# Choosing experts' tokens: gate bias and division by the sum moved from passes over 4096 tokens to columns and to the experts' answers

## The chip, the cores and the metric

The kernel runs on one core of one Trainium2 chip. The metric is the device time of one execution in microseconds (us); lower is better. The kernel before took 10838.91 us, the median of three runs (10834.52 to 10853.2). Everything is in float32.

## The reference, cut to what matters

Four images of 128 channels and 64 x 64 pixels pass through a convolution and scan layer, a convolution, an attention layer with an expert layer, and a second attention layer with a second expert layer. The change lies in the expert layers alone (`f2` and `f3` in the kernel). Each has 64 experts; every expert chooses 8 of the 4096 tokens of each image.

```
logits = einsum('bsd,ed->bse', x, gate_w) + gate_b          # x is the layer-normed token
probs  = softmax(logits, axis=1)                            # over the 4096 tokens
vals, idx = top_k(probs.transpose(0, 2, 1), 8)              # per image and expert
pooled = einsum('bked,bke->bed', gathered, topv)            # weighted sum of the 8 tokens
out    = two layers with gelu per expert, on pooled
outputs[token] += out * topv                                # added back to the 8 tokens
```

The softmax runs over tokens, so a gate bias, one number per expert, is the same for all the values that one softmax compares.

## The kernel before, in words

Images are kept as `xs[b]`, 128 channels (partitions) by 4096 tokens. `expert_ffn` works on pairs of images: a tile `picks[pr]` of 128 x 4096 holds, in its lower and upper 64 partitions, the 64 experts' logits for the two images of pair `pr`. For each of the two pairs there are three steps.

- `weigh(pr)` makes the layer norm's column scale `rs` and the logits, 512 tokens at a time, with TensorE (PE), ScalarE (ACT) and VectorE (DVE). Its last operation of each chunk writes `pick` (L1434).
- `choose(pr)` is nine operations of VectorE and one of ScalarE, each over the whole tile or over one column: add the gate bias (L1441), the eight largest (MAX8, L1443), the negated maximum `nmx` (L1445), the exponential with its sum `tot` on ScalarE (L1447), the reciprocal `rt` (L1449), the multiplication by `rt` (L1450), the eight largest again (L1452), a copy with these eight set to zero (L1454), the difference, which leaves the eight chosen weights (L1455), and their product with the token scale `rs` as `pick_rs` (L1456).
- `collect(pr)` turns `pick_rs` and the two images' tokens with TensorE transposes (L1468, tile `tok_t`), copies them out of PSUM (L1471 on VectorE, L1473 on ScalarE) and sums the weighted tokens into `pool`.

The order is `run(weigh(0)); choose(0); run(weigh(1), collect(0)); choose(1); run(collect(1))`; where two steps stand in one `run`, their chunks are interleaved. Then 16 groups of four experts follow (`hidden`, `turn_hidden`, `answer`, `place`), with 2 MB of weights per group, two groups held at a time, loaded by the SP queue (L1364, L1367). The sum of the answers, `out_ps`, is copied to `out_s` (L1555), and TensorE multiplies `out_s` with the chosen weights in `pick` and VectorE adds the result to the image (L1563). [...] Layer 3's attention lies between the two expert layers, and the output transfers follow the second.

## Time and profile before

One profiled execution took 10849.6 us by its own time; its span, from the first to the last instruction, is 10847.5 us. It is 10.7 us above the median of the three runs.

| stretch of the span (us) | work | length (us) | PE busy | DVE busy | TensorE clock |
|---|---|---|---|---|---|
| 0 to 9640 | layers 0 and 1, most of layer 2's attention | 9640 | 8190 | 7033 | 0.83 to 1.00 |
| 9769.0 to 9801.8 | f2, choose(0) | 32.8 | 0.0 | 27.2 | 0.54 |
| 9801.8 to 9868.1 | f2, weigh(1) and collect(0) | 66.3 | 59.5 | 38.0 | 0.97 |
| 9868.1 to 9899.6 | f2, choose(1) | 31.5 | 0.1 | 27.2 | 0.54 |
| 9927.0 to 10042.0 | f2, 16 expert groups | 115.0 | 94.5 | 16.3 | 0.79 |
| 10060.5 to 10482.0 | layer 3's attention | 421.5 | 300.4 | 252.9 | 0.91 |
| 10537.2 to 10570.0 | f3, choose(0) | 32.8 | 0.0 | 27.3 | 0.54 |
| 10570.0 to 10636.0 | f3, weigh(1) and collect(0) | 66.0 | 59.4 | 38.1 | 0.97 |
| 10636.0 to 10667.4 | f3, choose(1) | 31.4 | 0.0 | 27.2 | 0.54 |
| 10695.0 to 10815.0 | f3, 16 expert groups | 120.0 | 96.5 | 16.5 | 0.77 |

Busy times are sums over the instructions of one engine in the stretch. The TensorE clock is the share of full speed that was granted. In a timeline a row is: start, duration, engine, line, operation, output <- inputs, shapes, count, and in brackets how long the engine stood idle before it and what ended that.

### The profile page before, as it was taken

How to read it: one execution, taken by the hardware profiler on the slowest of the kernel's cores; microseconds unless marked ns; L12 is line 12 of the kernel's file. 1: busy time of each engine (PE TensorE's matmuls, PEld its weight loads, DVE VectorE, ACT ScalarE, POOL GpSimd, SP SyncE). 2: the span in 40 equal slices, each digit the busy share in tenths (PEclk: the TensorE clock that was granted, in tenths of full speed). 3: DMA queues.
4: the chain of work that ended last, by engine and by line, in shares of the span. 5: the costliest groups of instructions: out<-in, count | busy, mean ns of one | idle time of the engine just before them, and what ended most of it. 6: DMA issues, size and time to landing. Idle time of an engine off the chain costs nothing. (4 is left out here: it accounts for less than half of the span.)

```text
span 10847.5 us, 184105 instructions
## 1 busy us (share of the span) xinstructions
PE 9021.2 (83%) x71952; PEld 3473.1 (32%) x71952; DVE 7647.7 (71%) x8462; ACT 7513.2 (69%) x10317; POOL 5239.0 (48%) x3143
## 2 busy tenths in 40 slices
PE   5777778777866999978999978999978999976767
PEld 2123323322342333333333333333333333323433
DVE  2787677668856777767777767777767777754563
ACT  2665575565526999967999968999958999942431
POOL 1565555556634655645566635666635665520000
PEclk8788878878878999989999989999989999987888
DMA  3322322321212112222221122222222212223004
GB/s 81 88 70 56 89 73 55 86 75 50 62 60 49 34 33 36 37 68 44 33 38 35 33 71 42 38 35 34 33 75 42 35 34 33 33 89 105 6 17 140
DMA packets 524325, 581.58 MB, mean 54 GB/s; under 512 B 106232, under 2 KB 329536, under 8 KB 520896
## 3 DMA queue, kind: packets, MB, share of 16 engines
q1 hardware_dynamic: 523456, 569.81, 22.9%
q8 instruction: 568, 9.31, 0.4%
q14 instruction: 301, 2.47, 0.1%
HBM read 373.96 MB, written 76.55 MB: 42 GB/s over the span
## 5 line engine op out<-in xcount | busy, mean ns | idle before, releaser
L1208 ACT ACTIVATE ex<-score 128x1024 f32<-128x1024 f32 x5120 | 4934.2, 1033 | 469.8 <-PE score L90 180.1
L90 PE MATMUL ctx_ps<-ex,qt 128*32 128x512 f32 x20480 | 2719.4, 595 | 0.0
L1155 POOL TENSOR_TENSOR folded<-ex 128x1024 f32<-128x1024 f32 x704 | 1679.6, 2386 | 2074.2 <-ACT ex L1208 2054.2
L1214 DVE STREAM_TRANSPOSE turned<-ex 128x1024 f32<-128x1024 f32 x1536 | 1879.5, 1224 | 491.5 <-ACT ex L1208 428.1
L90 PE MATMUL acc_ps<-turned,turned_v 128*32 128x256 f32 x24576 | 1826.2, 388 | 181.4 <-DVE turned L1194 179.6
L1194 DVE STREAM_TRANSPOSE turned<-ex 128x1024 f32<-128x1024 f32 x1536 | 1854.0, 1207 | 0.0
L90 PE MATMUL score<-queries,keys 32*128 32x512 f32 x10240 | 1358.3, 496 | 140.7 <-ACT ex L1208 81.0
L687 DVE TENSOR_TENSOR_SCAN hs<-decay,carry,hs 128x512 f32<-128x512 f32 x1024 | 1252.8, 1266 | 197.3 <-ACT decay L686 183.0
L686 ACT ACTIVATE decay<-dt,a_neg 128x512 f32<-128x512 f32 x1024 | 700.9, 689 | 794.3 <-DVE hs L687 772.6
L90 PEld LDWEIGHTS score<-queries,keys 32*128 32x128 f32 x10240 | 524.3, 182 | 2196.0 <-issue 1666.2
L693 POOL TENSOR_TENSOR hs<-hs,c_sb 128x1024 f32<-128x1024 f32 x512 | 1205.1, 2375 | 43.5 <-DMA c_sb<-c_d 24.0
L1156 POOL TENSOR_TENSOR quarters<-folded 128x512 f32<-128x512 f32 x704 | 905.4, 1286 | 55.2
L90 PEld LDWEIGHTS acc_ps<-turned,turned_v 128*32 128x32 f32 x24576 | 561.6, 108 | 897.8 <-issue 555.8
L90 PEld LDWEIGHTS ctx_ps<-ex,qt 128*32 128x32 f32 x20480 | 684.5, 109 | 461.4 <-DVE ctx L1137 53.1
L90 PE MATMUL y_ps<-hs,pair 128*64 128x512 f32 x2048 | 652.3, 761 | 138.6 <-POOL hs L693 138.5
L683 DVE TENSOR_TENSOR hs<-dtx,b_ps 128x2048 f32<-128x2048 f32 x256 | 582.3, 2275 | 261.8 <-PE b_ps L90 177.1
L1137 DVE COPY ctx<-ctx_ps 128x512 f32<-128x512 f32 x256 | 177.0, 692 | 669.8 <-PE ctx_ps L90 669.8
L690 POOL COPY carry<-hs 128x4 f32<-128x4 f32 x256 | 59.8, 234 | 1028.0 <-DVE hs L687 990.5
L1027 POOL TENSOR_TENSOR turned_v<-v,quarter 128x1024 f32<-128x1024 f32 x192 | 459.5, 2394 | 17.4 <-ACT ex L1208 11.1
L1201 DVE TENSOR_REDUCE dacc<-quarters 128x2 f32<-128x512 f32 x704 | 453.2, 644 | 7.2 <-POOL quarters L1156 7.2
L90 PE MATMUL b_ps<-dbc,spread 32*128 32x512 f32 x512 | 322.3, 712 | 64.5 <-DVE hs L683 64.4
L1208 ACT ACTIVATION_READ_ACCUMULATOR ex<-score 128x1 f32 x1664 | 348.7, 210 | 0.0
(353 smaller groups left out, 9574.1 us busy)
## 6 DMA issues: line engine op xcount, KB each, us to landing
c_sb<-c_d SPq DMA_DIRECT2D x512, 128.0 KB
queries<-head_d SPq DMA_DIRECT2D x1024, 64.0 KB
keys<-head_d SPq DMA_DIRECT2D x1024, 64.0 KB
dt<-dt SPq DMA_DIRECT2D x128, 256.0 KB
dtx<-dtx SPq DMA_DIRECT2D x128, 256.0 KB
w<-in_L_ffn_weight SPq DMA_DIRECT2D x32, 1024.0 KB
w<-in_L_ffn_weight SPq DMA_DIRECT2D x128, 256.0 KB
under<-xp SPq DMA_DIRECT2D x384, 66.0 KB
```

The source lines that it names most:

```text
L90: self.nc.tensor.matmul(out, lhsT, rhs, start=start, stop=stop)
L683: nc.vector.tensor_tensor(hs, dtx2, bb.unsqueeze(1).to_broadcast([P, NQ, CH]), ALU.mult)
L686: nc.scalar.activation(ex, dt2[:, q, :], AF.Exp, scale=a_neg[:, q, g : g + 1])
L687: nc.vector.tensor_tensor_scan(hs[:, q, :], ex, hs[:, q, :], carry[:, g, q : q + 1], ALU.mult, ALU.add)
L693: nc.gpsimd.tensor_tensor(at, at, cs.unsqueeze(1).to_broadcast([P, 2, CH]), ALU.mult)
L1027: nc.gpsimd.tensor_tensor(t, v.unsqueeze(2).to_broadcast([P, 4 * BT, 4, HD]), quarter.unsqueeze(1).to_broadcast([P, 4 * BT, 4, HD]), ALU.mult,
L1155: nc.gpsimd.tensor_tensor(hs, exs[:, :, 0], exs[:, :, 1], ALU.add)
L1156: nc.gpsimd.tensor_tensor(qs, hs[:, :, 0 : CH // 2], hs[:, :, CH // 2 :], ALU.add)
L1194: nc.vector.transpose(*upright)
L1201: nc.vector.tensor_reduce(at, qs, AX.X, ALU.add)
L1208: nc.scalar.activation(ex, sps[p], AF.Exp, scale=scale, accum_out=dacc[:, j, h, t : t + 1] if summed else None)
L1214: nc.vector.transpose(*upright)
```

## The change

Three things are edited, all in `expert_ffn`. The pass that adds the gate bias over 128 x 4096 goes; the bias enters the column `nmx` instead, which becomes -(top + bias) by one operation with two steps and then has the bias added by a new one. The pass that multiplies 128 x 4096 exponentials by `rt` goes; the second MAX8, the replacement and the difference work on undivided exponentials. `rt` is kept per pair (in the pool `tok`, under a name per pair) and is multiplied in at two places: in `pick_rs`, whose product of two tensors becomes a product with a column and a tensor, and at the copy of the answers' sum into `out_s`.

```diff
         def choose(pr):
 
             pb, rs = picks[pr], parts[pr]
-            nc.vector.tensor_scalar(pb, pb, gate_b, None, ALU.add)
             top = work.tile([P, 8], F32, name="top")
             nc.vector.max(top, pb)
             nmx = work.tile([P, 1], F32, name="nmx")
-            nc.vector.tensor_scalar(nmx, top[:, 0:1], -1.0, None, ALU.mult)
+            nc.vector.tensor_scalar(nmx, top[:, 0:1], gate_b, -1.0, ALU.add, ALU.mult)
+            nc.vector.tensor_tensor(nmx, nmx, gate_b, ALU.add)
             tot = work.tile([P, 1], F32, name="tot")
             nc.scalar.activation(pb, pb, AF.Exp, bias=nmx, accum_out=tot)
-            rt = work.tile([P, 1], F32, name="rt")
+            rt = tok.tile([P, 1], F32, name=f"rt{pr}")
             nc.vector.reciprocal(rt, tot)
-            nc.vector.tensor_scalar(pb, pb, rt, None, ALU.mult)
+            scales.append(rt)
             top = work.tile([P, 8], F32, name="top")
             nc.vector.max(top, pb)
             ws = parts[pr] = tok.tile([P, L], F32, name="pick_rs")
             nc.vector.match_replace(ws, top, pb, 0.0)
             nc.vector.tensor_tensor(pb, pb, ws, ALU.subtract)
-            nc.vector.tensor_tensor(ws, pb, rs, ALU.mult)
+            nc.vector.scalar_tensor_tensor(ws, pb, rt, rs, ALU.mult, ALU.mult)
...
             os_ = work.tile([P, P], F32, name="out_s")
-            nc.vector.tensor_copy(os_, ops[pr])
+            nc.vector.tensor_scalar(os_, ops[pr], scales[pr], None, ALU.mult)
```

On every other engine and queue the instructions and their order are those of before; on VectorE only the rows shown differ. The tiles of the pool `work` in the two expert layers lie 64 bytes further on.

## The prediction

> **What bounds the kernel here.** I read the waits of TensorE (PE) after layer 2 first, then the stretches of the four choices, then the first of them instruction by instruction, then the chain of work that ended last, and last the rows that price the new operations. The waits, as engine, line and awaited engine, then total us, times, longest:

> ```profile
> PE tok_t L1468 <- DVE pick_rs L1456: 134.1, 4, 33.7
> PE hid_ps L90 <- DMA w<-in_L_ffn_weight: 39.3, 13, 5.1
> ```

> PE stands 33 us at each of four places until `pick_rs` is written. By stretch (busy PE, PEld, DVE, ACT, POOL, granted clock, DMA share, GB/s), nothing runs beside VectorE (DVE) there but ScalarE's exponential:

> ```profile
> 9769.00:9801.80 32.80, 0.00 (x0) 0.03 (x1) 27.21 (x10) 5.08 (x3) 0.00 (x0) 0.54 0.00 0
> 9868.10:9899.60 31.50, 0.08 (x1) 0.08 (x2) 27.23 (x11) 3.80 (x2) 0.00 (x0) 0.54 0.00 0
> ```

> The first choice in order of time; the reader is to see that each row starts when the one before ends, that the only gap is ScalarE's, and that PE starts 0.14 us after the last row ends:

> ```profile
> 9769.00 2.35 DVE L1441 TENSOR_SCALAR pick<-pick,gate_b 128x4096 f32<-128x4096 f32 x1
> 9771.39 4.43 DVE L1443 MAX8 top<-pick 128x8 f32<-128x4096 f32 x1
> 9775.85 0.15 DVE L1445 TENSOR_SCALAR nmx<-top 128x1 f32<-128x1 f32 x1
> 9781.20 0.16 DVE L1449 RECIPROCAL rt<-tot 128x1 f32<-128x1 f32 x1 [5.20 <-ACT pick L1447]
> 9781.40 2.35 DVE L1450 TENSOR_SCALAR pick<-pick,rt 128x4096 f32<-128x4096 f32 x1
> 9783.79 4.43 DVE L1452 MAX8 top<-pick 128x8 f32<-128x4096 f32 x1
> ...
> 9797.23 4.42 DVE L1456 TENSOR_TENSOR pick_rs<-pick,rs 128x4096 f32<-128x4096 f32 x1
> 9801.80 1.08 PE L1468 MATMUL tok_t<-ident,pick_rs 128*128 128x128 f32 x4 [33.70 <-DVE pick_rs L1456]
> ```

> The chain that ended last passes through the two later choices in the same rows; of the last one:

> ```profile
> 10636.03 2.36 DVE pick L1441
> 10638.42 4.44 DVE top L1443
> 10643.07 3.81 ACT pick L1447 x2
> 10647.10 2.37 DVE pick L1450
> 10649.49 4.44 DVE top L1452
> ```

> The chain that is shown begins at 10062.7, so for the two choices of f2 the place on the path is inferred from PE's wait, not read. So the choices' DVE work is serial, and what it loses should move all that follows.

> **Removed.** Two passes per choice. From start to start, L1441 takes 9771.39 - 9769.00 = 2.39 us and L1450 9783.79 - 9781.40 = 2.39; the last choice gives 2.39 for both too. Per choice 4.78, four choices 19.12 us. L1450 gone starts MAX8 straight after the reciprocal, which already waits for ScalarE, so no new wait appears. L1441 gone makes the first MAX8 wait for L1434, on the same engine, just before it. The wait for `gate_b`'s transfers moves to `nmx`; they landed before PE's first matmul of the stage, over 50 us earlier.

> **Added, per choice.**

> - `nmx` gets a column as its scalar instead of a number. The 128x1 rows with a column (layer norm's `gn_v`, median 219 ns) and without (`gn_off`, 158 ns) differ by 0.06 us; I take that. Ends 0 and 0.06.
> - A new 128x1 sum of two columns. `gn_d`, a TENSOR_TENSOR of this size, has median 144 ns; the reciprocal's row shows 0.04 between its end and the next start (9781.20 + 0.16 to 9781.40). So 0.18; ends 0.14 and 0.22. ScalarE's exponential, and in the first choice of each layer its 1.28 us table load, wait for `nmx` and start 0.24 later.
> - L1456 becomes a pass with a column and two tensors. No row has it at 4096. At 128x512 from PSUM, `nrm` (two tensors) is 691 ns and `ln_rs` (column and two tensors) 751 at the median: +0.06. From SBUF the nearest is `eq` at 128x256, median 485 ns. The two-tensor rows at 512 and 4096 elements give (4425 - 691) / 3584 = 1.042 ns an element, an estimate, and 691 - 512 x 1.042 = 158 ns fixed; `eq` has 485 - 256 x 1.042 = 218 fixed. Again +0.06. The lower end is -0.01 (`e_q` with a number, 681 ns, against 691); the upper end is `eq`'s slowest single row, 2511 ns, +2.0 us as a stall. I take +0.06, the median of both forms.

> Together +0.30, so 4.48 us net per choice and 17.92 for four.

> **Moved.** `out_s` is scaled while it leaves PSUM: a 128x128 copy of 292 ns becomes a column operation. SBUF rows of 128x128 give 217 ns with a number (`group_mean`) and 280 with a column (`ksh`): +0.06. Of the two per layer only the first is on the path; the second lies under DVE's 1.00 us wait for the first `y_ps`. Two layers: +0.12; ends 0 and +0.24. PE, which waits for `out_s`, is the one delayed.

> Other engines keep their order. Expert weights of groups 0 and 1 are in place before the choice (DMA share 0.00 in the rows above), and group 2 is requested after group 0 is used, so these transfers move with the chain. No DMA or SP instruction passes another.

> **What is late next.** After each choice PE restarts at a low clock:

> ```profile
> 9804.00:9805.00 1.00, 1.00 (x4) 0.72 (x3) 0.00 (x0) 0.73 (x2) 0.00 (x0) 0.50 0.00 0
> 9805.00:9806.00 1.00, 1.00 (x2) 0.00 (x0) 0.00 (x0) 0.98 (x2) 0.00 (x0) 0.64 0.00 0
> 9806.00:9807.00 1.00, 1.00 (x17) 0.85 (x16) 0.71 (x1) 0.66 (x2) 0.00 (x0) 1.00 0.00 0
> ```

> From 9801.8 it holds 0.50 until about 9805.7, that is 3.9 us; after the other three choices 5.1, 3.6 and 5.2. The longest and shortest differ by 1.6 us, which at half the clock is 0.8 of work; if four restarts fall otherwise, that is +-3.2. I take 0, since nothing in the rows says which sign. [...]

> **Sum.** -17.92 + 0.12 = -17.8 us. The profiled execution's own time is 10849.6 (span 10847.5 and 2.1 around it); it would become 10831.8. It stands 10.7 above the median shown, so the median would go from 10838.91 to 10821.1, or -0.164%. What a measurement of this kernel can tell from no change is about 0.2%, 21.7 us: the gain is just inside it.

> **Rivals.**

> 1. *The expert groups fall better or worse.* Work after the choice starts earlier, and the 16 groups alternate between the weights' transfer and PE at a changing clock:

> ```profile
> 9927.00:10042.00 115.00, 94.53 (x1092) 41.66 (x1091) 16.33 (x35) 11.11 (x18) 0.00 (x0) 0.79 0.81 257
> 10695.00:10815.00 120.00, 96.53 (x1091) 42.15 (x1091) 16.46 (x35) 11.11 (x18) 0.00 (x0) 0.77 0.77 246
> ```

> The same work took 5.0 us more in f3. If f3 fell as f2 does: -22.8, 10816.1. If f2 fell as f3 does: -12.8, 10826.1. For it: both stretches are a chain of transfer and PE. Against: both start after the same rigid shift, and no row ties the 5 us to the start.

> 2. *The passes were hidden*, or the change buys nothing because something else ends the choice: 10838.9. Against it is the 33 us of PE, DMA share 0.00 and ScalarE's 5.1 us.

> 3. *The pass with a column and two tensors runs slow: slower than before.* If not a stall but the element rate of `eq`'s slowest row held, 2511 / 256 x 4096 = 40.2 us per pass, the sum would be -17.8 + 4 x 35.7 = +125, 10963.9. It decides from 8.9 us per pass (4.48 + 4.42). For it: that row is the same form. Against it: the median is 485, the slow rows lie in layer 0, where GpSimd (POOL) works too, and POOL is at 0.00 in the choices. With only one 2.0 us stall per pass the time is 10829.

> **How the numbers follow.** Rigid shift 0.72; rival 1 better 0.12, worse 0.07; rival 2 0.04; rival 3 0.05. The three runs and the profiled one spread from 10834.5 to 10853.2, half of that 9 us, so a reading of the rigid case lies past -21.7 in about a third: 0.25 of its 0.72. Faster 0.25 + 0.12 = 0.37; same 0.47 + 0.07 + 0.04 = 0.58; slower 0.05. The rigid case alone: 10811 to 10831. The range goes to both ends of rival 1 with a spread of 9 to 10 us on top: 10807 to 10836; it leaves out rivals 2 and 3.

> **What would show it.** In the changed trace: each choice 4.5 us shorter (28.3 and 27.0 us), PE's wait for `pick_rs` 134.1 - 17.9 = 116.2 us, `pick_rs` at 4.48 us, `nmx` as two rows of 0.21 and 0.14, `out_s` at 0.35, both MAX8 at 4.43. I am wrong if `pick_rs` is far over 4.5, if the expert groups move by more than 5 us, or if the time up to 9640, where nothing is changed, differs by as much as the gain.

## The result and the profile after

The changed kernel takes 10824.39 us, the median of 20 runs (10804.07 to 10834.14); the kernel before, run beside it, 10844.96 us (10834.2 to 10857.38, 20 runs). The ratio of after to before is 0.998, with a 95% interval from 0.9973 to 0.9987: a gain of about 20.6 us, between 14 and 29. The forecast was 17.8 us.

The profiled execution took 10826.6 us, span 10824.5. Its span is 23.0 us shorter than that of before, and that is not all the change. What the edits did is read from the choices themselves. First the waits of PE after layer 2, as before (total, times, longest):

```profile
PE tok_t L1469 <- DVE pick_rs L1457: 115.7, 4, 29.1
```

The wait has gone from 134.1 to 115.7 us, 18.4 less; 116.2 was forecast. The first choice of the changed kernel in order of time (from the new row of `nmx` on, the lines of the code are one further on):

```profile
9758.95 4.43 DVE L1443 MAX8 top<-pick 128x8 f32<-128x4096 f32 x1
9763.42 0.21 DVE L1445 TENSOR_SCALAR nmx<-top,gate_b 128x1 f32<-128x1 f32 x1
9763.67 0.16 DVE L1446 TENSOR_TENSOR nmx<-nmx,gate_b 128x1 f32<-128x1 f32 x1
9769.02 0.16 DVE L1450 RECIPROCAL rt<-tot 128x1 f32<-128x1 f32 x1 [5.20 <-ACT pick L1448]
9769.10 4.41 DVE L1453 MAX8 top<-pick 128x8 f32<-128x4096 f32 x1
...
9782.53 4.49 DVE L1457 SCALAR_TENSOR_TENSOR pick_rs<-pick,rt,rs 128x4096 f32<-128x4096 f32 x1
9787.16 1.09 PE L1469 MATMUL tok_t<-ident,pick_rs 128*128 128x128 f32 x4 [29.10 <-DVE pick_rs L1457]
```

The two passes of 2.35 us are gone, `nmx` is two rows, `pick_rs` has grown from 4.42 to 4.49 us, and PE still starts 0.14 us after the last row (0.06 us in the second choice of a layer, before and after). The last choice in the chain that ended last:

```profile
10616.27 4.44 DVE top L1443
10621.17 3.81 ACT pick L1448 x2
10625.17 4.34 DVE top L1453
```

By stretch, in the columns of the prediction's table of stretches:

```profile
9758.90:9787.10 28.20, 0.00 (x0) 0.00 (x0) 22.71 (x10) 5.08 (x3) 0.00 (x0) 0.57 0.00 0
9853.00:9879.90 26.90, 0.04 (x1) 0.04 (x1) 22.73 (x10) 3.80 (x2) 0.00 (x0) 0.54 0.00 0
```

From row to row of VectorE's timelines, in all the profiled executions (lengths in us; a choice runs from the end of the last L1434 row to the end of `pick_rs`, the expert groups from `pooled` to `out_s`; e1 to e7 are the experiments below):

| | before | after | e1 | e2 | e3 | e4 | e5 | e6 | e7 |
|---|---|---|---|---|---|---|---|---|---|
| span's start to f2's first copy (`gate`) | 9716.2 | 9708.1 | 9720.7 | 9718.1 | 9708.2 | 9706.4 | 9714.9 | 9703.9 | 9705.5 |
| f2, choice 0 | 32.68 | 28.10 | 30.55 | 30.22 | 37.46 | 28.80 | 19.30 | 28.10 | 19.44 |
| f2, choice 1 | 31.36 | 26.77 | 29.23 | 28.90 | 36.14 | 27.74 | 17.98 | 26.77 | 18.10 |
| f2, expert groups | 113.4 | 117.6 | 113.6 | 112.9 | 115.3 | 116.0 | 116.3 | 115.7 | 115.6 |
| end of f2 to f3's `gate` | 421.6 | 420.8 | 426.3 | 421.6 | 419.0 | 419.0 | 422.8 | 421.7 | 420.1 |
| f3, choice 0 | 32.69 | 28.10 | 30.56 | 30.23 | 37.47 | 28.79 | 19.31 | 28.09 | 19.43 |
| f3, choice 1 | 31.35 | 26.77 | 29.23 | 28.89 | 36.14 | 27.74 | 17.97 | 26.77 | 18.11 |
| f3, expert groups | 118.3 | 120.2 | 114.9 | 113.3 | 116.7 | 113.5 | 116.1 | 110.9 | 116.8 |

The four choices are 4.58, 4.59, 4.59 and 4.58 us shorter, together 18.3. Of the other 4.7 us by which the two spans differ, 8.1 lie ahead of f2, where nothing is edited, and the two stretches of expert groups give 6.1 back; the rest is scattered over unedited steps. The first row shows how far unedited work moves from one execution to the next: 9703.9 to 9720.7.

### The profile page after: what moved, and what is told of

Its sections match the earlier page's. It is cut to its first block, busy times and chain, and to the rows that moved or that the text cites. A ratio compares the mean times of both kernels' runs of the same rounds, so it can differ in the third digit from the quotient of the medians.

```text
span 10824.5 us, 184101 instructions
## 1 busy us (share of the span) xinstructions
PE 9004.5 (83%) x71952; PEld 3462.0 (32%) x71952; DVE 7631.8 (71%) x8458; ACT 7513.9 (69%) x10317; POOL 5240.4 (48%) x3143
## 3 DMA queue, kind: packets, MB, share of 16 engines
q14 instruction: 301, 2.47, 0.1%
## 5 line engine op out<-in xcount | busy, mean ns | idle before, releaser
L90 PE MATMUL ctx_ps<-ex,qt 128*32 128x512 f32 x20480 | 2719.1, 595 | 0.0
L90 PE MATMUL acc_ps<-turned,turned_v 128*32 128x256 f32 x24576 | 1826.2, 388 | 182.0 <-DVE turned L1194 180.2
L90 PE MATMUL score<-queries,keys 32*128 32x512 f32 x10240 | 1358.3, 496 | 141.1 <-ACT ex L1208 81.0
L90 PEld LDWEIGHTS score<-queries,keys 32*128 32x128 f32 x10240 | 524.3, 182 | 2196.4 <-issue 1666.2
L90 PEld LDWEIGHTS acc_ps<-turned,turned_v 128*32 128x32 f32 x24576 | 561.6, 108 | 898.6 <-issue 556.2
L90 PEld LDWEIGHTS ctx_ps<-ex,qt 128*32 128x32 f32 x20480 | 684.1, 109 | 461.3 <-DVE ctx L1137 53.2
L90 PE MATMUL y_ps<-hs,pair 128*64 128x512 f32 x2048 | 641.1, 749 | 136.3 <-POOL hs L693 136.1
L1027 POOL TENSOR_TENSOR turned_v<-v,quarter 128x1024 f32<-128x1024 f32 x192 | 459.7, 2395 | 17.8 <-ACT ex L1208 11.2
L90 PE MATMUL b_ps<-dbc,spread 32*128 32x512 f32 x512 | 318.1, 703 | 72.5 <-DVE hs L683 72.5
```

The lines of the kernel that those rows point to most:

```text
L90: self.nc.tensor.matmul(out, lhsT, rhs, start=start, stop=stop)
L1027: nc.gpsimd.tensor_tensor(t, v.unsqueeze(2).to_broadcast([P, 4 * BT, 4, HD]), quarter.unsqueeze(1).to_broadcast([P, 4 * BT, 4, HD]), ALU.mult,
```

## The experiments

The theory: a choice is one serial chain of VectorE while the rest of the core waits, so the time moves by the start-to-start time of what is edited there and by nothing else. The rivals: that the gain has a part beyond the choices (20.6 against 18.3); that the expert groups answer to when they start; and that the pass with a column can be slow beside GpSimd.

**One half alone: the bias (e1).**

```diff
-            nc.vector.tensor_scalar(pb, pb, gate_b, None, ALU.add)
...
-            nc.vector.tensor_scalar(nmx, top[:, 0:1], -1.0, None, ALU.mult)
+            nc.vector.tensor_scalar(nmx, top[:, 0:1], gate_b, -1.0, ALU.add, ALU.mult)
+            nc.vector.tensor_tensor(nmx, nmx, gate_b, ALU.add)
```

> The kernel before with only the gate bias moved into the column nmx; the division by the sum stays a pass over 128 x 4096. Theory (each choice is a serial chain of VectorE, so the time moves by the start-to-start time of what is edited): per choice 2.39 us less for the bias pass, 0.06 more for the column in nmx and 0.20 for the new column operation, so 2.13 us; the first choice of a layer goes from 32.7 us (end of L1434 to end of pick_rs) to 30.5, the second from 31.4 to 29.2, and the execution is 8.5 us shorter (ratio 0.9992). Rival (the removed passes free work beyond the choices, so that the gain of 20.6 us has 2.3 us more than the choices' own 18.3): half of the surplus, 9.7 us, with the expert groups of this trace shorter than 117 us. Rival (only the division's pass mattered): ratio 1.000 and the choices unchanged.

Measured: ratio 0.9996, interval 0.9987 to 1.0005, median 10839.72 (11 runs) against 10844.22 (27 runs), 4.5 us less. The interval holds the theory's 0.9992, no gain, and the rival's 9.7 us alike. The trace tells more: the choices lost 2.13, 2.13, 2.13 and 2.12 us, 8.5 in all, as the theory had it. The rival that only the division mattered falls. The expert groups, 113.6 and 114.9 us, are shorter than 117, as the rival of a surplus wanted, but so they are where nothing at all is edited (e6 below). In this version the second MAX8 still reads what L1450 writes:

```profile
9783.40 0.16 DVE L1449 RECIPROCAL rt<-tot 128x1 f32<-128x1 f32 x1 [5.20 <-ACT pick L1447]
9783.60 2.35 DVE L1450 TENSOR_SCALAR pick<-pick,rt 128x4096 f32<-128x4096 f32 x1
9785.99 4.43 DVE L1452 MAX8 top<-pick 128x8 f32<-128x4096 f32 x1
```

**The other half alone: the division (e2).** The edit is the rest of the change: `rt` into `pick_rs` and `out_s`, the bias as a pass.

> The changed kernel with the gate bias as a pass over 128 x 4096 again; only the division by the sum is moved to columns and answers. Theory of the serial chain: per choice 2.39 us less, 0.06 more for the column in pick_rs, and 0.14 less because the second MAX8 no longer reads what the reciprocal makes and starts while that still runs: 2.47 us, four choices 9.9, out_s 0.1 more for two layers: 9.8 us shorter than before (ratio 0.9991); choices 30.2 and 28.9 us. The two halves then add to 18.3. Rival of the surplus: 11 us. If the overlap of MAX8 with the reciprocal came from the bias and not from the division, the second MAX8 starts 0.20 us after the reciprocal's start here, not 0.08.

Measured: ratio 0.9995, interval 0.9987 to 1.0004, median 10836.88 (11 runs), 7.3 us below 10844.22. Again the interval separates nothing; the choices lost 2.46, 2.46, 2.46 and 2.46 us, 9.8, against 9.9 expected. With the bias' 8.5 the halves add to the whole's 18.3. The overlap belongs to the division:

```profile
9783.07 0.16 DVE L1450 RECIPROCAL rt<-tot 128x1 f32<-128x1 f32 x1 [5.20 <-ACT pick L1448]
9783.15 4.41 DVE L1453 MAX8 top<-pick 128x8 f32<-128x4096 f32 x1
```

MAX8 starts 0.08 us after the reciprocal's start, before its 0.16 us are over, where L1450 above, which reads `rt`, starts 0.20 after it; and its row is 4.41 instead of 4.43. So a removed dependence gave 0.12 us in addition to the removed pass.

**The other way: two more passes (e3).**

```diff
             nc.vector.tensor_scalar(pb, pb, gate_b, None, ALU.add)
+            nc.vector.tensor_scalar(pb, pb, gate_b, None, ALU.add)
+            nc.vector.tensor_scalar(pb, pb, gate_b, None, ALU.add)
```

> The kernel before with the bias pass three times instead of once, that is two more passes per choice (it adds the bias three times, and a constant per expert changes nothing in a softmax). Theory of the serial chain: 2 x 2.39 x 4 = 19.1 us longer than before (ratio 1.0018), choices 37.5 and 36.1 us, and PE's wait for pick_rs 134.1 + 19.1 = 153.2 us. Rival (the passes lie partly under other work, so that only some of their time shows): less than 15 us. Rival (a shift of the restarts and expert groups costs or gives several us by itself): more than 24 or less than 14 us, and the expert groups of this trace outside 113 to 121 us.

Measured: ratio 1.002, interval 1.0011 to 1.0029, median 10861.15 (11 runs), 16.9 us above 10844.22; the interval is 12 to 31 us. The choices grew by 4.78, 4.78, 4.78 and 4.79 us, 19.1, and PE waited for exactly what was forecast:

```profile
PE tok_t L1470 <- DVE pick_rs L1458: 153.2, 4, 38.5
```

Passes put in cost what passes taken out gave, pass for pass: 2.39 us each. The expert groups, 115.3 and 116.7, stay within the band that the expectation gave to the theory; the rival of a shift that costs or gives several us, outside 14 to 24, is not excluded by the time alone.

**A working GpSimd beside the choice (e4).**

```diff
+        busy = cst.tile([P, CH], F32, name="busy")
+        nc.gpsimd.memset(busy, 0.0)
...
             nc.vector.max(top, pb)
+            nc.gpsimd.tensor_tensor(busy[:, 0:8], top, busy[:, 8:16], ALU.mult)
+            for _ in range(16):
+                nc.gpsimd.tensor_tensor(busy, busy, busy, ALU.mult)
```

> The changed kernel with GpSimd kept busy during each choice: after the first MAX8 one 128x8 and sixteen 128x512 products of two tensors on a tile of zeros that nothing else reads. This measures the disputed price, a pass with a column and two tensors beside a working GpSimd, for which layer 0's rows gave 485 ns at the median and 2511 ns once. Rival of the slow pass: the passes of VectorE that have two tensors (the difference and pick_rs) rise from 4.42 and 4.49 us by 2 us or more each while the one-tensor MAX8 and the replacement stay at 4.41, the choices are 4 us or more longer than 28.1 and 26.8, and the execution is 16 us or more longer than the changed kernel. If GpSimd waits instead: VectorE's rows stay within 0.1 us, and GpSimd's 128x512 product, 1.2 us in layer 0, becomes longer. If neither gives way: both rows stay, choices 28.1 and 26.8 us.

One execution: 10820.46 us, which by itself says little. The choices are 0.7 us (choice 0) and 1.0 us (choice 1) longer than those of the changed kernel, 3.3 in all, not 16. Two groups of VectorE and then GpSimd's products in two stretches of the first choice: beside MAX8, the exponential and the replacement, and beside the two passes with two tensors (count: shortest/median/longest in ns, first and last start):

```profile
L1461 DVE TENSOR_TENSOR pick<-pick,pick_rs x4: 4472/4576/4683, 9778.1 to 10633.0; 128x4096 f32<-128x4096 f32 x4
L1462 DVE SCALAR_TENSOR_TENSOR pick_rs<-pick,rt,rs x4: 5143/5144/5144, 9782.6 to 10637.7; 128x4096 f32<-128x4096 f32 x4
```

```profile
L1448 POOL TENSOR_TENSOR busy<-busy x13: 1038/1039/1040, 9763.9 to 9777.3; 128x512 f32<-128x512 f32 x13
...
L1448 POOL TENSOR_TENSOR busy<-busy x3: 1039/5101/5102, 9777.3 to 9783.6; 128x512 f32<-128x512 f32 x3
```

Both give way, which none of the three expectations said. GpSimd's product, 1.04 us beside passes with one tensor, took 5.10 when it began in a pass with two: in this choice from 9778.38 to 9783.48 and from 9783.56 to 9788.66, both times to 0.90 us past the end of that pass. VectorE's passes grew by 0.05 to 0.26 us (the difference) and by 0.66 (`pick_rs`); in this choice 0.19 and 0.86 us of a product were left when they began.

The 2511 ns row of layer 0, on which rival 3 rested, also stands beside a GpSimd product. In the trace of before:

```profile
2280.88 4.66 POOL L693 TENSOR_TENSOR hs<-hs,c_sb 128x1024 f32<-128x1024 f32 x2
2283.30 2.51 DVE L455 SCALAR_TENSOR_TENSOR eq<-sm,cl,before 128x256 f32<-128x256 f32 x1
2285.49 1.36 POOL L487 TENSOR_TENSOR x<-pe,xp 128x512 f32<-128x512 f32 x1
```

`eq` starts while a GpSimd product of 2.35 us runs, with 2.24 us of it left, and ends 0.27 us after it (at 2285.81 against 2285.54). The two other slow rows, of 2508 and 2291 ns, end 0.29 and 0.28 us after such a product; the five `eq` rows that start with GpSimd idle take 452 to 485 ns. So in these rows the price of rival 3 was no more than what was left of one GpSimd instruction, 2.1 us of 2.24 there and 0.66 of 0.86 here, and no element rate.

**The changed kernel again, unedited (e6).**

> The changed kernel once more, unedited: what two executions of one program differ by. Theory of the serial chain: the four choices are within 0.05 us of 28.1, 26.8, 28.1 and 26.8, while stretches that no edit touches move by several us with either sign: the start of f2 by up to 14 us from 9708, the expert groups between 113 and 121 us, layer 3 by a few us. Ratio to before 0.998. Rival (the expert groups' 117.6 and 120.2 us of the first trace belong to the change): both groups within 1 us of these values again.

Measured: ratio 0.9982, interval 0.9973 to 0.999, median 10825.18 (11 runs), 17.0 us below 10842.2. The choices repeat to 0.01 us, and f2 starts 4.2 us earlier. The expert groups of f3 took 120.2 us in one execution of this program and 110.9 in the other (stretches that hold them; busy PE, PEld, DVE, ACT, POOL, clock, DMA share, GB/s), the first trace and then the second:

```profile
10671.60:10791.80 120.20, 95.64 (x1088) 41.93 (x1088) 16.04 (x34) 10.27 (x17) 0.00 (x0) 0.76 0.78 245
```

```profile
10667.60:10778.40 110.80, 89.92 (x1088) 39.99 (x1088) 15.99 (x33) 10.26 (x17) 0.00 (x0) 0.82 0.84 266
```

The same instructions, 9.4 us apart, with a granted clock of 0.76 and 0.82. So the rival that gave the longer groups of the first trace to the change falls. The 110.9 also lies below the 113 to 121 that was expected: the scatter was taken too small. What decides between the lengths was not separated.

**Further on the same road: a threshold (e5).** Since only VectorE's rows count there, three more of them were taken out.

```diff
-            top = work.tile([P, 8], F32, name="top")
-            nc.vector.max(top, pb)
+            nc.scalar.activation(top, top, AF.Exp, bias=nmx)
             ws = parts[pr] = tok.tile([P, L], F32, name="pick_rs")
-            nc.vector.match_replace(ws, top, pb, 0.0)
-            nc.vector.tensor_tensor(pb, pb, ws, ALU.subtract)
+            nc.vector.scalar_tensor_tensor(pb, pb, top[:, 7:8], pb, ALU.is_ge, ALU.mult)
             nc.vector.scalar_tensor_tensor(ws, pb, rt, rs, ALU.mult, ALU.mult)
```

> The changed kernel, carried further by what the first runs showed (a choice costs exactly its VectorE rows from start to start, whatever else is idle). The second MAX8, the replacement and the difference go; the eight largest logits of the first MAX8 pass through the same exponential as a 128x8 column block, and one pass keeps the exponentials that are not below the eighth and sets the others to zero (where two values tie for the eighth place it would keep both). Theory of the serial chain: from the reciprocal's start to the end of pick_rs 18.0 us become 0.25 for the small exponential plus 4.52 and 4.49, 9.3 in all; the choices go from 28.1 and 26.8 to 19.4 and 18.1 us, 34.8 us less than the changed kernel and 53.1 less than the kernel before: about 10791, ratio 0.9951. Rival (the chip's expert groups or restarts take back what the choices give, since they start earlier): ratio above 0.9965, with the expert groups longer than 121 us. Rival (a comparison with a column is slower than a product): the new pass far over 4.5 us.

Measured: 10792.28 us (5 runs) against 10842.2 (15 runs of the kernel before, beside it), 49.9 us less; ratio 0.9949, interval 0.9935 to 0.9962, where 10791 and 0.9951 were forecast. The choices are 19.3 and 18.0 us, 53.5 us less than before in all, and the expert groups 116.3 and 116.1. The first of the two passes starts 0.04 us after the small exponential ends and 0.19 after the reciprocal's start, and the comparison costs what a product costs:

```profile
9777.66 0.28 ACT L1452 ACTIVATE top<-top,nmx 128x8 f32<-128x8 f32 x1
9777.79 0.16 DVE L1450 RECIPROCAL rt<-tot 128x1 f32<-128x1 f32 x1 [5.20 <-ACT pick L1448]
9777.98 4.49 DVE L1454 SCALAR_TENSOR_TENSOR pick<-pick,top 128x4096 f32<-128x4096 f32 x1
9782.50 4.49 DVE L1455 SCALAR_TENSOR_TENSOR pick_rs<-pick,rt,rs 128x4096 f32<-128x4096 f32 x1
```

Here the time itself decides: the expected 53.1 us lies in the interval (41 to 70), and the rival's 0.9965 outside.

**And in halves (e7).**

```diff
-            nc.vector.scalar_tensor_tensor(pb, pb, top[:, 7:8], pb, ALU.is_ge, ALU.mult)
-            nc.vector.scalar_tensor_tensor(ws, pb, rt, rs, ALU.mult, ALU.mult)
+            for at in (slice(0, L // 2), slice(L // 2, L)):
+                nc.vector.scalar_tensor_tensor(pb[:, at], pb[:, at], top[:, 7:8], pb[:, at], ALU.is_ge, ALU.mult)
+                nc.vector.scalar_tensor_tensor(ws[:, at], pb[:, at], rt, rs[:, at], ALU.mult, ALU.mult)
```

> The threshold version with its two passes cut into halves of 2048 tokens, so that TensorE's first transposes need only the first half of pick_rs. VectorE does both halves of the first pass before those of the second. Theory of the serial chain: two more starts of 0.25 us each make the choice 0.5 us longer on VectorE, but TensorE starts 2.4 us before its end; the first copy of tok_t comes 0.8 us earlier per choice and the step behind it ends 0.8 to 1.9 us earlier, 3 to 8 us in all, 10783 to 10788. Rival (the step behind is bound by VectorE's copies, which still wait for the second half): no gain, or 2 us lost.

Measured: 10777.28 us (5 runs), ratio 0.9939, interval 0.9927 to 0.9952, the fastest of all, 15.0 us below the uncut version and below the expected 10783 to 10788, though its interval overlaps that of the uncut version. The loop writes the two passes of each half in turn; the trace shows both halves of the first pass ahead of the second's, as the expectation has it. On VectorE the halves cost 0.12 to 0.14 us per choice, not 0.5, because the second half of a pass does not read the first and begins before it ends (two rows of 2.35 span 4.61). PE starts with one half of `pick_rs` done, and the first copy of `tok_t` follows the last pass at once instead of 1.2 to 1.3 us after it. From the reciprocal to the end of the step behind, the four choices gained 1.2, 2.2, 2.7 and 3.0 us over the uncut version, 9.0 together, a little over the expected 3 to 8. Part of the spread is that step's own: from the end of `pick_rs` it took 65.6 to 67.4 us after a choice 0 and 28.7 to 29.8 after a choice 1 in the eight other executions. Here it took 64.8, 63.6, 27.0 and 26.5, less than any of these, so the rival of no gain falls.

## Why the prediction was right

- *The mechanism.* A rigid shift, choice by choice, with PE at once behind it: the traces show it in both directions, in each half of the change alone, the two more passes and the threshold; the times show it for the two more passes and the threshold, whose forecasts lie inside intervals that do not reach zero.
- *Removed, 4.78 per choice.* 2.39 for each pass, as read from start to start before; e3 gave 4.78 for two.
- *Added, 0.30 per choice.* From `nmx`'s start to ScalarE's, 0.22 us became 0.47 (9763.42 to 9763.89): +0.25, taken as 0.24. `pick_rs` was 4485 ns at all four places against the 4.48 forecast; rival 3's slow rate did not occur: GpSimd was at 0.00 in the choices, and no `eq` row that started with GpSimd idle took more than 485 ns. That `eq` gave the same +0.06 as the rows from PSUM was partly luck: its median of 485 is over all eight rows, the three slow ones among them; the five that start with GpSimd idle have 455, which would have given +0.03.
- *What was missed.* "L1450 gone starts MAX8 straight after the reciprocal" was too careful: MAX8 overlaps it, 0.12 us a choice. This is why the choices gave 18.3 and not 17.9.
- *Moved.* The first `out_s` of each layer took 350 ns against the forecast 0.35, and PE started on it 0.40 us after it began, where 0.35 was the figure before; the second (341 ns) lies hidden.
- *What is late next.* The restarts of PE cost nothing on balance: 3.9, 5.2, 3.6 and 5.3 us at the low clock, 0.50, before (the prediction read two of them 0.1 short), 3.1, 5.9, 5.2 and 3.9 after, 18.0 and 18.1 together. That the 0 was met so closely is luck: over the nine executions the four sum to 16.8 to 20.0 us.
- *Rival 1* was real as a scatter and wrong as an answer to the change: groups from 110.9 to 120.2 us in executions of one program. *Rival 2* fell with the first trace.
- *The signs of being wrong.* None came: `pick_rs` stayed under 4.5 us, the expert groups moved by 4.2 and 1.9 us, and the start of f2, with nothing edited ahead of it, by 8.1, less than half the gain.
- *The time.* The forecast 10821.1 stands 3.3 us from the median, partly by luck: the median of before was 10844.96, 6.1 above the three runs that the forecast was counted from, and the gain 2.8 more than forecast, so that two errors go against each other. The difference of 20.6 includes the 18.3 that the traces show, and 2.3 that the interval of 14 to 29 cannot tell from scatter; the same program gave 17.0 in e6, on the other side of 18.3. The gain came out inside the 0.2%, barely, as the rigid case had it; with 20 runs of each kernel its interval, 14 to 29 us, still does not reach zero. e1 and e2 show the same limit: 8.5 and 9.8 us, certain in the traces, are within noise in the times.

## What to carry to other kernels

Where one engine works alone and all others wait, add up its rows from start to start: that sum is what the stretch loses, to a tenth of a microsecond here even where the measured time could not show it. What lies behind the stretch shifts with it, but fell by several microseconds either way from one execution to the next. A factor that is constant along a row belongs in the column operand of a pass that has to be made anyway, since a column cost 0.06 us here and a pass 2.39. And the same sum told what to take out next: the threshold version took 53.5 us out of the choices where this change took 18.3.

## What the runs showed of the hardware

```profile
9790.00:9790.50 0.50, 0.50 (x2) 0.08 (x1) 0.00 (x0) 0.50 (x1) 0.00 (x0) 0.78 0.00 0
```

- *A step of that grid that PE had not filled was followed by the full clock.* The step in which PE starts again and the one behind it, first in e2 (f3, choice 0), then in e3 (the same place):

```profile
10561.96:10565.38 3.42, 2.65 (x13) 2.69 (x14) 1.31 (x2) 0.59 (x1) 0.00 (x0) 0.50 0.00 0
10565.38:10568.79 3.41, 3.41 (x19) 1.85 (x18) 0.71 (x1) 2.19 (x3) 0.00 (x0) 0.50 0.02 5
```

```profile
10575.65:10579.07 3.42, 2.74 (x13) 2.77 (x14) 1.22 (x2) 0.59 (x1) 0.00 (x0) 0.50 0.00 0
10579.07:10582.48 3.41, 3.41 (x26) 1.95 (x25) 0.71 (x1) 2.47 (x4) 0.00 (x0) 1.00 0.02 5
```

With 2.65 us of PE's work the clock stayed low for one step more, with 2.74 it rose. All 36 restarts of the nine traces fall in with this: the five first steps with 2.74 us or more were followed by the full clock, the 31 with 2.65 or less were not (in before they had 0.23 to 1.88 us and in after 0.50, 1.81 and 2.52; 3.06, the first of after, was followed by it). So these two restarts, which began within 0.1 us of each other in their steps, spent 6.1 and 2.7 us at the low clock.
- *A row of VectorE that does not read the row before it began earlier than one that does*: 0.08 us after the start of a 0.16 us reciprocal (after, e2), against 0.20 (before, e1); in e7 two halves of 2.35 us spanned 4.61, not 4.7.
- *A GpSimd product and a pass of VectorE with two tensors that ran side by side took longer, and the one that began second lost less than what was left of the first*: in e4 a product of 1.04 us took 5.10 with 4.20 us of such a pass left, and `pick_rs` 5.14 instead of 4.49 with 0.86 us of a product left; in layer 0 of before an `eq` row that takes 0.45 to 0.49 us by itself took 2.51 with 2.24 us of a product left. So the shorter instruction lost more in e4, 4.06 us against 0.66.
